# Neighbourhood attention on one core: position tables loaded in four pieces, the second image on GpSimd's queue, and a new order of the first work

## The chip, the cores and the metric

One core of a Trainium2 chip runs the whole kernel. The metric is device time in microseconds of that core, here the median of three runs. The core has a matrix engine (PE, with its weight loads as PEld), VectorE (DVE), ScalarE (ACT), GpSimd (POOL) and SyncE (SP), which work side by side, each through its own list of instructions in order. SP, ACT and POOL can also issue DMA transfers; a transfer's issue stands in the list of the engine that issues it.

## What is computed

Two images of 128 channels and 64 x 64 pixels, float32. After a group norm comes a block with neighbourhood attention (7 x 7 window, four heads of 32), then an attention over all 4096 tokens, then a long convolution by spectral filters. The change touches only the beginning of the first block. Cut to that:

```python
x = _gn(x)                                        # 32 groups, per image
y = _ln(x.transpose(0, 2, 3, 1), g1, be1)
qkv = (y @ qkv_w.T + qkv_b)                       # 3 x 4 heads x 32
attn = einsum('bnhwd,bnhwijd->bnhwij', q, Kw)     # 7 x 7 keys round each pixel
attn = attn + rpb[:, bih, biw][None]              # relative position, rpb is (4, 13, 13)
attn = softmax(attn over the 49 keys)
out = einsum('bnhwij,bnhwijd->bnhwd', attn, Vw)
...                                               # projection, two more norms, a small MLP, residuals
...                                               # attention over tokens, spectral filters
```

`rpb` holds, for each head, one number for each of 13 x 13 relative positions.

## The kernel before

**Tiling.** An image is cut into eight bands of eight rows (512 pixels); a band into eight tiles of 8 x 8 pixels, taken two at a time as four units u0 to u3. A unit computes, for each head, the scores of 2 x 64 pixels against a window of 14 x 14 = 196 keys (piece `S`, L505), adds a table and takes a minimum on DVE (piece `t`, L518), exponentials on ACT (piece `e`, L528), transposes the result on PE (`T`, L541), copies it out of PSUM (`c`, L548) and multiplies it with V on PE (`V`, L563). Two bands of keys and values must be there before the first scores.

**The table** (`tab`, L241) has, for six kinds of place in the image and four heads, 128 x 196 numbers: a mask (`mask`, loaded at L283) less the position numbers (`base`). `table` (L254) makes one of them; kind 0 is made on DVE, the others on POOL. `base` comes out of `flipped` (L246): `rev` holds, in 64 partitions, one for each pixel of a tile, the head's numbers shifted by the pixel's row and column; one matmul of 64 x 400 with a reversed identity turns the order of the partitions round, and ACT copies the result. `rev` is loaded straight from `rpb_pad`, a zero-padded copy of `rpb` in DRAM with rows of 128 numbers (`RPW`), by sixteen DMAs at L284 to L292: for each of the eight pixel rows one for heads 1 to 3 and one for head 0, all in runs of 20 numbers. POOL zeroes two parts of it first (L281, L282). `rev` lies in the space of `cm[0]`, `base` and `mask` in that of `tok[0]`; both are written with other things later.

**V.** ACT copies a band's V out of PSUM (piece `p.vc`, L470); SP stores it to DRAM in eight DMAs (`vd`, L475) and loads it back, as windows of 14 x 14 keys, in four DMAs for each unit (`windows`, L484 to L493). Those buffers (`vw`) are six units deep.

**The order.** Each engine's order is the order in which the program emits the pieces. Every piece of every band has a due time in `PLAN`, with 2300 between bands; the pieces are sorted by it. What comes first is written out by hand in `FIRST` (L72): its names get the times -1000, -999 and so on. `gn` is the group norm of the first image, `p.xg0` band 0's normalised pixels, `p.tok0` their transposes, `p.bn`, `p.pw`, `p.zd`, `p.nb`, `p.za`, `p.tr`, `p.zT` the layer norm, `p.q`, `p.k`, `p.v` the linears, `p.qT`, `p.kT`, `p.vc` their copies; `w` and `wd` prepare the weights, `f0` to `f3` are `flipped` of each head, `tab0` to `tab3` the tables of kind 0, `tab` those of kinds 1, 4 and 5. `behind` (L746) makes biases and weights that are used only behind the attention; its four steps lie at 150, 500, 850 and 1200 (L790). `second` (L793) loads the second image on ACT's queue, four DMAs of 512 KB, at 1000. The first image is loaded by SP in four DMAs at L126. The second image's own group norm begins at 2 x 2300 + 50 (L799).

Within a manual schedule the four compute engines keep this order; SP's DMAs follow the order of their program too.

Of the kernel before, what the change touches and what calls it, by code (L numbers as in the profile page):

```python
# [8 lines left out]
F32 = mybir.dt.float32  # L9
# [5 lines left out]
P = 128  # L15
# [5 lines left out]
HEADS, DH, KW = 4, 32, 7  # L21
# [9 lines left out]
W_QKV, W_PROJ, W_1, W_2, W_3 = 0, 384, 512, 640, 768  # L31
V_G1, V_BE1, V_G2, V_BE2, V_G3, V_BE3, V_G4, V_BE4, V_QB, V_KB, V_BL3 = range(11)
R_VB, R_PROJ, R_BL1, R_BL2 = range(4)
RPW = 128


QT, WN, NTAB = 8, 14, 20
# [2 lines left out]
BAND = QT * GW  # L40


RPR = NTAB + 1

# [23 lines left out]


FIRST = (  # L72
    "gn p.xg0 p.xg1 p.tok0 p.tok1 w p.bn0 p.bn1 p.pw0 p.pw1 p.zd0 p.nb0 p.za0 p.tr0 p.zd1 p.nb1 p.za1 wd p.xg2 p.zT0 f0"
    " p.tr1 f1 p.v0 p.q0 p.k0 p.zT1 p.vc0 p.qT0 tab0 p.kT0 f2 f3 tab p.v1 p.k1 p.q1 tab1 p.vc1 p.kT1 p.qT1 tab2 tab3"
).split()
PHW = P + TH

# [15 lines left out]
def kernel(  # L93
# [16 lines left out]
    nc = tc.nc  # L110
# [12 lines left out]
    xa = [xp.tile([P, T], F32, tag=f"xa{b}", name=f"xa{b}") for b in range(NB)]  # L123
    xin = x.rearrange("b c h w -> b c (h w)")
    for c in range(4):
# [3 lines left out]
    tt, tok, cm = [None, None], [None, None], [None, None]  # L129
# [4 lines left out]
    space = tok[0].rearrange("p n c -> p (n c)")  # L134
    base = space[:, 0 : HEADS * NTAB * NTAB].rearrange("p (h n m) -> p h n m", h=HEADS, n=NTAB)
    mask = space[:, HEADS * NTAB * NTAB : HEADS * NTAB * NTAB + 6 * KEYS].rearrange("p (c k) -> p c k", k=KEYS)
    rev = cm[0][0 : QT * QT, 0 : HEADS * RPR * NTAB].rearrange("p (h n m) -> p h n m", h=HEADS, n=RPR)

    ident = const.tile([P, P], F32, name="ident")
    make_identity(nc, ident)  # L140
# [4 lines left out]
        out=flip, in_=flip, compare_op=ALU.not_equal, fill=1.0, base=1 - QT * QT, pattern=[[0, 2], [1, QT * QT]],  # L145
# [73 lines left out]
    with l0a:  # L219
# [10 lines left out]
        vdram = l0a.enter_context(tc.tile_pool(name="l0_dram", bufs=1, space=bass.MemoryType.DRAM))  # L230
# [10 lines left out]
        tab = big.tile([P, 6, HEADS, KEYS], F32, name="tab")  # L241
        def l0_bank(kind=0):
            pool, tag = rings[kind]
            return pool.tile([P, 512], F32, tag=tag, name="bank")

        def flipped(h):  # L246
            pb = l0_bank()
            nc.tensor.matmul(
                pb[:, 0 : NTAB * NTAB], lhsT=flip.rearrange("p a q -> p (a q)"),
                rhs=rev[:, h, 0:NTAB].rearrange("p n m -> p (n m)"), start=True, stop=True,  # L250
            )
            nc.scalar.copy(base[:, h].rearrange("p n m -> p (n m)"), pb[:, 0 : NTAB * NTAB])

        def table(ci, h, eng):  # L254
            n0 = (6, 0, 3)[ci // 2]
            for hp, m0 in ((slice(0, 64), 6), (slice(64, P), 0)) if ci % 2 == 0 else ((slice(0, P), 3),):
                eng.tensor_tensor(
                    tab[hp, ci, h].rearrange("p (n m) -> p n m", m=WN),
                    mask[hp, ci].rearrange("p (n m) -> p n m", m=WN),
                    base[hp, h, n0 : n0 + WN, m0 : m0 + WN], ALU.subtract,  # L260
                )
# [9 lines left out]
            out=gavg, in_=gavg, compare_op=ALU.is_ge, fill=0.0, base=0,  # L271
# [3 lines left out]
            out=gavg, in_=gavg, compare_op=ALU.is_ge, fill=0.0, base=3,  # L275
            pattern=[[4, 32], [0, 4]], channel_multiplier=-1,
        )
        gavg = gavg.rearrange("p g r -> p (g r)")


        nc.gpsimd.memset(rev[:, 0].rearrange("p n m -> p (n m)"), 0.0)  # L281
        nc.gpsimd.memset(rev[:, HEADS - 1, NTAB], 0.0)  # L282
        nc.sync.dma_start(out=mask, in_=nc.inline_tensor(_window_masks(), "window_masks").ap())  # L283
        for r in range(QT):  # L284
            lo = 6 - min(r, 6)
            src = bass.AP(
                rpb_pad.tensor, (RPR + r - 6) * RPW + 50, [[1, QT], [RPW, (HEADS - 1) * RPR - r // 7], [1, NTAB]]
            )
            rows_ = rev[r * QT : (r + 1) * QT].rearrange("p h n m -> p (h n) m")
            (nc.scalar if r % 3 == 2 else nc.sync).dma_start(out=rows_[:, RPR : HEADS * RPR - r // 7], in_=src)  # L290
            src = bass.AP(rpb_pad.tensor, (lo + r - 6) * RPW + 50, [[1, QT], [RPW, RPR - lo], [1, NTAB]])
            nc.scalar.dma_start(out=rows_[:, lo:RPR], in_=src)  # L292
        wg = w_sb
        cb = wp.tile([P, 5], F32, name="cb")
        C_Q, C_K, C_V, C_1, C_3 = range(5)
# [38 lines left out]
        def group_norm(b):  # L334
            xb = xa[b]
            gst = mp.tile([P, 8, 6], F32, tag="gst", name="gst", bufs=1)
            gmv = mp.tile([P, 2], F32, tag="gmv", name="gmv", bufs=1)
            for c in range(8):
                nc.vector.bn_stats(gst[:, c, :], xb[:, c * 512 : (c + 1) * 512])
                if c % 2:  # L340
                    yield
            nc.vector.bn_aggr(gmv, gst.rearrange("p a s -> p (a s)"))
            yield
            gm = mp.tile([P, 1], F32, tag="gm", name="gm", bufs=2)
            gv = mp.tile([P, 1], F32, tag="gv", name="gv", bufs=1)
            pb = l0_bank()
            nc.tensor.matmul(pb[:, 0:1], lhsT=gavg, rhs=gmv[:, 0:1], start=True, stop=True)
            nc.vector.tensor_copy(gm, pb[:, 0:1])
            nc.vector.tensor_tensor(gv, gmv[:, 0:1], gm, ALU.subtract)
            nc.vector.tensor_tensor(gv, gv, gv, ALU.mult)  # L350
            nc.vector.tensor_tensor(gv, gv, gmv[:, 1:2], ALU.add)
            yield
            pb = l0_bank()
            nc.tensor.matmul(pb[:, 0:1], lhsT=gavg, rhs=gv, start=True, stop=True)
            grs = mp.tile([P, 1], F32, tag="grs", name="grs", bufs=2)
            rsqrt(grs, pb[:, 0:1], 1e-5)
            norms[b] = gm, grs
            yield
# [413 lines left out]
        events = []  # L772
        for k, (b, g) in enumerate(order):
            t = {}
            for name, at in PLAN.items():
                if name[0] == "k" and b == 0:
                    continue

                at = FIRST.index(f"{name}{k}") - 1000 if f"{name}{k}" in FIRST else at + k * PERIOD
                events.append((at, k, name, lambda f=pieces[name], t=t, b=b, g=g: f(t, b, g)))  # L780
        for name, f in (
            ("gn", lambda: [None for _ in group_norm(0)]), ("w", weights), ("wd", weights_kept),
            *((f"f{h}", lambda h=h: flipped(h)) for h in range(HEADS)),
            *((f"tab{h}", lambda h=h: table(0, h, nc.vector)) for h in range(HEADS)),
            ("tab", lambda: [table(ci, h, nc.gpsimd) for ci in (1, 4, 5) for h in range(HEADS)]),
        ):
            events.append((FIRST.index(name) - 1000, None, "", f))
        for i in range(8):
            events.append((2 * PERIOD + 600 * i, None, "", lambda ci=2 + i // 4, h=i % 4: table(ci, h, nc.gpsimd)))
        rest_ = behind()  # L790
        for i in range(4):
            events.append((150 + 350 * i, None, "", lambda: next(rest_)))
        def second():  # L793
            for c in range(4):
                nc.scalar.dma_start(out=xa[1][:, c * 1024 : (c + 1) * 1024], in_=xin[1, :, c * 1024 : (c + 1) * 1024])

        events.append((1000, None, "", second))

        gn1 = group_norm(1)  # L799
        for i in range(7):  # L800
# [597 lines left out]
def _window_masks():  # L1398

    import numpy as np  # L1400

    def seen(offset):

        q, k = np.arange(QT)[:, None], np.arange(WN)[None, :]
        lo = np.clip(offset + q - 3, 0, WN - KW)
        return (k >= lo) & (k < lo + KW)

    m = np.zeros((2, QT, QT, 6, WN, WN), np.float32)
    for ci in range(6):
        rows_ = seen((0, 6, 3)[ci // 2])  # L1410
        for ab in range(2):
            cols = seen(((0, 6), (3, 3))[ci % 2][ab])
            m[ab, :, :, ci] = np.where(rows_[:, None, :, None] & cols[None, :, None, :], 0.0, -MASKED)
    return m.reshape(P, 6, KEYS)
# [75 lines left out]
```

## Time and profile before

| | us |
|---|---|
| median of 3 runs | 2242.70 |
| lowest, highest | 2241.91, 2243.04 |
| the profiled execution | 2241.68 |
| its span in the profile | 2240.0 |
| PE busy | 2174.1 (97%) |
| PEld busy | 1344.1 (60%) |
| DVE busy | 940.5 (42%) |
| ACT busy | 780.6 (35%) |
| POOL busy | 276.2 (12%) |

The profiled execution lies 1.0 us below the median, and its span 1.7 us below its own time. The page of the profile gives busy times over the whole span, then the same in 40 slices, the DMA queues, the chain of work that ended last, and the costliest groups of instructions. A line of a group or of the timeline reads: start in us, duration in us, engine, source line, operation, output <- inputs with their shapes, the number of instructions, and in brackets the idle time of the engine just before and what ended it. "SPq" and "ACTq" are the DMA issues in an engine's own list; the time of a group of issues runs from the first to the end of the last, with waits between them. A table of stretches gives, for a stretch of time, its length and each engine's busy time in it with the number of instructions, then PE's granted clock as a share of full speed, the mean busy share of the 16 DMA engines and the GB/s that they moved.

The first 350 us or so are the neighbourhood attention of both images; it ends in the token attention of image 0, then come the rest of the attention and the filters.

### The profile page before, as it was taken

To read this page: it belongs to the slowest core of one execution; us is meant where nothing else is said; L and a number is where in the kernel's file an instruction comes from. 1 tells how busy PE (TensorE), PEld (TensorE's weight loads), DVE (VectorE), ACT (ScalarE), POOL (GpSimd) and SP (SyncE) were. 2 spreads that over 40 slices of the span, in tenths; PEclk is the share of its full clock that TensorE was granted. 3 is DMA by queue.
4 is the path that set the end of the run, shared out by engine and by line. 5 is a ranking of instruction groups with operands and counts; after the bars stand their busy time and mean duration, and the time that the engine had idled before them with its cause. 6 is when DMAs were issued, how large, how long until landed. Compare 5 with 4: busy or idle time off the path is not lost.

```text
span 2240.0 us, 31648 instructions
## 1 busy us (share of the span) xinstructions
PE 2174.1 (97%) x11888; PEld 1344.1 (60%) x11888; DVE 940.5 (42%) x3046; ACT 780.6 (35%) x1908; POOL 276.2 (12%) x353
## 2 busy tenths in 40 slices
PE   5899998999999999999999999999999999999998
PEld 3677765544454444544544447767677676767677
DVE  4799985434443346433333351222222323232323
ACT  2889883222332223222222332222322323232322
POOL 3377874200000000000000000000000000000000
PEclk8999998999999999999999999999999999999999
DMA  4222212011000016100000132212212122221101
GB/s 119 65 62 60 62 53 51 1 66 52 24 24 24 19 41 175 33 24 23 2 24 24 47 94 55 59 44 54 59 42 56 45 53 50 49 52 46 43 7 76
DMA packets 174810, 109.53 MB, mean 49 GB/s; under 512 B 26049, under 2 KB 159809, under 8 KB 174146
## 3 DMA queue, kind: packets, MB, share of 16 engines
q1 hardware_dynamic: 171818, 105.24, 18.0%
q10 hardware_dynamic: 2840, 2.27, 0.4%
q8 instruction: 94, 1.54, 0.3%
q14 instruction: 58, 0.48, 0.1%
HBM read 72.87 MB, written 34.60 MB: 48 GB/s over the span
## 4 chain that ended last, share of the span: by engine, by line
PE 86%; DVE 6%; POOL 3%; DMA 2%; ACT 1%; SPq 1%; issue 1%; DVEq 0%; ACTq 0%; POOLq 0%
PE acc L1316 25%; PE pc L1304 13%; PE bank L897 10%; PE own L925 10%; PE other L950 8%; PE bank L911 4%; PE py L1343 2%; PE bank L331 2%; PE bank L188 2%; PE bank L1042 2%; PE bank L1010 1%; PE bank L541 1%; DMA st<-in_m_minus_dram 1%; PE bank L505 1%; PE po L563 1%
## 5 line engine op out<-in xcount | busy, mean ns | idle before, releaser
L1305 DVE COPY y<-pc 128x512 f32<-128x512 f32 x320 | 221.4, 692 | 351.6 <-PE pc L1304 347.9
L904 ACT ACTIVATE e<-bank 128x512 f32<-128x512 f32 x288 | 171.8, 597 | 549.9 <-PE bank L897 415.2
L897 PE MATMUL bank<-cm 128*128 128x512 f32 x576 | 299.7, 605 | 1.4 <-DVE y L652 1.4
L1316 PE MATMUL acc<-y,mpl 128*128 128x256 f32 x1280 | 292.1, 382 | 0.0
L1316 PE MATMUL acc<-y,mmi 128*128 128x256 f32 x1280 | 288.0, 379 | 0.0
L1304 PE MATMUL pc<-ct,ut 64*128 64x512 f32 x1280 | 285.2, 595 | 0.9 <-issue 0.9
L1316 PEld LDWEIGHTS acc<-y,mpl 128*128 128x128 f32 x1280 | 238.2, 190 | 59.3 <-issue 29.6
L1316 PEld LDWEIGHTS acc<-y,mmi 128*128 128x128 f32 x1280 | 242.6, 190 | 32.6
L1305 ACT COPY y<-pc 128x512 f32<-128x512 f32 x320 | 204.5, 639 | 87.3 <-PE pc L1304 87.3
L925 PE MATMUL own<-et,tok 128*128 128x512 f32 x448 | 227.0, 593 | 1.9 <-DVE part L914 1.9
L950 PE MATMUL other<-e,tok 128*128 128x512 f32 x448 | 228.6, 592 | 0.0
L914 DVE CUSTOM_DVE_ANT_0 et<-bank,one 128x512 f32<-128x512 f32 x224 | 145.6, 687 | 166.0 <-PE bank L911 165.9
L1304 PEld LDWEIGHTS pc<-ct,ut 64*128 64x128 f32 x1280 | 121.5, 187 | 145.8 <-issue 140.6
L1322 ACT COPY ob<-acc 128x256 f32<-128x256 f32 x40 | 23.8, 595 | 431.2 <-PE acc L1316 431.2
L925 PEld LDWEIGHTS own<-et,tok 128*128 128x128 f32 x448 | 84.5, 190 | 109.8 <-issue 71.8
L950 PEld LDWEIGHTS other<-e,tok 128*128 128x128 f32 x448 | 85.1, 190 | 106.6 <-issue 105.7
L897 PEld LDWEIGHTS bank<-cm 128*128 128x128 f32 x576 | 96.2, 194 | 74.9 <-issue 46.1
L1355 DVE TENSOR_TENSOR xa<-py,xa 128x512 f32<-128x512 f32 x32 | 22.1, 691 | 281.4 <-PE py L1343 281.4
L911 PEld LDWEIGHTS bank<-ident,e 128*128 128x128 f32 x896 | 102.9, 141 | 56.5 <-issue 42.1
L160 POOL TENSOR_TENSOR ln_rs<-ln_rs,mhalf 128x4 f32<-128x4 f32 x24 | 24.3, 1011 | 848.0 <-DVE ln_rs L159 848.0
L528 ACT ACTIVATE p<-p,mn 128x196 f32<-128x196 f32 x256 | 114.4, 449 | 20.8 <-DVE mn L518 13.4
L911 PE MATMUL bank<-ident,e 128*128 128x128 f32 x896 | 117.3, 274 | 0.0
(199 smaller groups left out, 2311.1 us busy)
## 6 DMA issues: line engine op xcount, KB each, us to landing
ut<-us SPq DMA_DIRECT2D x80, 256.0 KB
us<-ub SPq DMA_DIRECT2D x64, 256.0 KB
vw<-vd SPq DMA_DIRECT2D x256, 49.0 KB
ct<-gs SPq DMA_DIRECT2D x160, 72.0 KB
ct<-gs SPq DMA_DIRECT2D x160, 64.0 KB
gs<-sum SPq DMA_DIRECT2D x20, 256.0 KB
vd<-v SPq DMA_DIRECT2D x128, 32.0 KB
st<-in_m_plus_dram SPq DMA_DIRECT2D x16, 256.0 KB
```

The source lines that it names most:

```text
L188: nc.tensor.transpose(ps[:, j * P : (j + 1) * P], src[:, j, :], ident)
L331: nc.tensor.matmul(pl, lhsT=wg[:, lo : lo + P], rhs=zT, start=True, stop=True)
L528: nc.scalar.activation(p, p, AF.Exp, bias=t[name + "mn"][:, h : h + 1], scale=-1.0, accum_out=t["den"][:, u, h : h + 1],)
L897: nc.tensor.matmul(ps, lhsT=cm[b][:, n * P : (n + 1) * P], rhs=cm[b][:, chunk(c)], start=True, stop=True)
L904: nc.scalar.activation(e, ps, AF.Exp, bias=0.0, scale=ASCALE, accum_out=part[:, n, c : c + 1])
L911: nc.tensor.transpose(pt[:, k * P : (k + 1) * P], es[k][:, m * P : (m + 1) * P], ident)
L914: nc.vector.tensor_tensor_reduce(et, pt, one, 1.0, 0.0, ALU.mult, ALU.add, part[:, n, a : a + 1])
L925: nc.tensor.matmul(own, lhsT=tok[b][:, n, :], rhs=e, start=first, stop=last)
L950: nc.tensor.matmul(other, lhsT=tok[b][:, 4 * CHUNKS[a] + j, :], rhs=es[j], start=(j == 0), stop=(j == 3))
L1304: nc.tensor.matmul(pc, lhsT=ut[fp, b, par, :], rhs=cv_[fp], start=True, stop=True)
L1305: (nc.scalar.copy if f else nc.vector.tensor_copy)(y[:, 4 * f : 4 * f + 4, :, par, b * 2 * FB + q : (b + 1) * 2 * FB : 2], pc.rearrange("p ...
L1316: nc.tensor.matmul(acc, lhsT=(mmi if l else mpl)[:, k, :], rhs=y[:, 1::2, k, ::-1, :] if l else y[:, 0::2, k, :, :], start=(l == 0 and k = ...
```

## The change

1. *Table loads.* The padded table has rows of 70 numbers instead of 128, and 22 rows for a head instead of 21. The six rows ahead of it are needed too, so that DRAM space `rpb` of (6 + 88) x 70 numbers is filled by two DMAs, DRAM to DRAM: its first six rows with the table's first six, as filler, then the whole table. Then one DMA for each head loads `rev[h]`: partition (row, column) reads 1350 numbers in one run from `row * 70 + column` on. The matmul of `flipped` picks 20 runs of 20 numbers out of them, with a step of 70. The four pieces of `rev` lie in `tt[0]` (heads 0 and 3) and `cm[0]` (heads 1 and 2). POOL's two memsets are gone. All six DMAs are on ACT's queue; before, six of the sixteen were on SP's.
2. *Second image.* `second` is issued from POOL's queue, as `x1` in `FIRST`, after `p.pw1`, and no longer from ACT's at 1000.
3. *Order.* `f0` and `f1` stand right after `w`, `f2` after `p.zT0`, `f3` after `p.tr1`; `tab` right after `f3`; `tab0` to `tab2` before `p.kT0`, `tab3` after it. The steps of `behind` lie at 900, 1200, 1500 and 1800.

```diff
-RPW = 128
+RPW = 70
-RPR = NTAB + 1
+RPR = NTAB + 2
+RLEN = (NTAB - 1) * RPW + NTAB

 FIRST = (
-    "gn p.xg0 p.xg1 p.tok0 p.tok1 w p.bn0 p.bn1 p.pw0 p.pw1 p.zd0 p.nb0 p.za0 p.tr0 p.zd1 p.nb1 p.za1 wd p.xg2 p.zT0 f0"
-    " p.tr1 f1 p.v0 p.q0 p.k0 p.zT1 p.vc0 p.qT0 tab0 p.kT0 f2 f3 tab p.v1 p.k1 p.q1 tab1 p.vc1 p.kT1 p.qT1 tab2 tab3"
+    "gn p.xg0 p.xg1 p.tok0 p.tok1 w f0 f1 p.bn0 p.bn1 p.pw0 p.pw1 x1 p.zd0 p.nb0 p.za0 p.tr0 p.zd1 p.nb1 p.za1 wd p.xg2"
+    " p.zT0 f2 p.tr1 f3 tab p.zT1 p.v0 p.q0 p.k0 p.vc0 p.qT0 tab0 tab1 tab2 p.kT0 tab3 p.v1 p.k1 p.q1 p.vc1 p.kT1 p.qT1"
 ).split()

-    rev = cm[0][0 : QT * QT, 0 : HEADS * RPR * NTAB].rearrange("p (h n m) -> p h n m", h=HEADS, n=RPR)
+    place = tt[0].rearrange("p n c -> p (n c)")[0 : QT * QT, 3 * P :]
+    rev = [place[:, 0 : NTAB * RPW], *(cm[0][0 : QT * QT, h * RLEN : h * RLEN + NTAB * RPW] for h in range(2))]
+    rev.append(place[:, NTAB * RPW : 2 * NTAB * RPW])

-                rhs=rev[:, h, 0:NTAB].rearrange("p n m -> p (n m)"), start=True, stop=True,
+                rhs=rev[h].rearrange("p (n w) -> p n w", w=RPW)[:, :, 0:NTAB], start=True, stop=True,

-        nc.gpsimd.memset(rev[:, 0].rearrange("p n m -> p (n m)"), 0.0)
-        nc.gpsimd.memset(rev[:, HEADS - 1, NTAB], 0.0)
         nc.sync.dma_start(out=mask, in_=nc.inline_tensor(_window_masks(), "window_masks").ap())
-        for r in range(QT):
-            lo = 6 - min(r, 6)
-            src = bass.AP(
-                rpb_pad.tensor, (RPR + r - 6) * RPW + 50, [[1, QT], [RPW, (HEADS - 1) * RPR - r // 7], [1, NTAB]]
-            )
-            rows_ = rev[r * QT : (r + 1) * QT].rearrange("p h n m -> p (h n) m")
-            (nc.scalar if r % 3 == 2 else nc.sync).dma_start(out=rows_[:, RPR : HEADS * RPR - r // 7], in_=src)
-            src = bass.AP(rpb_pad.tensor, (lo + r - 6) * RPW + 50, [[1, QT], [RPW, RPR - lo], [1, NTAB]])
-            nc.scalar.dma_start(out=rows_[:, lo:RPR], in_=src)
+        rpb = vdram.tile([(6 + HEADS * RPR) * RPW], F32, name="rpb")
+        flat = rpb_pad.rearrange("h r w -> (h r w)")
+        nc.scalar.dma_start(out=rpb[0 : 6 * RPW], in_=flat[0 : 6 * RPW])
+        nc.scalar.dma_start(out=rpb[6 * RPW :], in_=flat)
+        for h in range(HEADS):
+            src = bass.AP(rpb.tensor, rpb.offset + h * RPR * RPW + 50, [[RPW, QT], [1, QT], [1, RLEN]])
+            nc.scalar.dma_start(out=rev[h][:, 0:RLEN], in_=src)

+        def second():
+            for c in range(4):
+                nc.gpsimd.dma_start(out=xa[1][:, c * 1024 : (c + 1) * 1024], in_=xin[1, :, c * 1024 : (c + 1) * 1024])

-            ("tab", lambda: [table(ci, h, nc.gpsimd) for ci in (1, 4, 5) for h in range(HEADS)]),
+            ("x1", second), ("tab", lambda: [table(ci, h, nc.gpsimd) for ci in (1, 4, 5) for h in range(HEADS)]),

-            events.append((150 + 350 * i, None, "", lambda: next(rest_)))
-        def second():
-            for c in range(4):
-                nc.scalar.dma_start(out=xa[1][:, c * 1024 : (c + 1) * 1024], in_=xin[1, :, c * 1024 : (c + 1) * 1024])
-
-        events.append((1000, None, "", second))
+            events.append((900 + 300 * i, None, "", lambda: next(rest_)))
```

The matrix work is the same before and after, and so are the stores and window loads of V. Behind the first lines of the changed kernel its line numbers are one higher in the attention (L506 for the scores, L519, L529, L542, L564).

## The prediction

> **What bounds the kernel now.** I read the page first: PE is busy 2174.1 us of 2240.0 (97%), so a change that takes no matmul away can only win where PE is idle. The slices put PE's idle time at the head of the program. The table of stretches shows it:
>
> ```profile
> core 0: us, PE busy (x) PEld busy (x) DVE busy (x) ACT busy (x) POOL busy (x), PEclk, DMA share, GB/s
> ...
> 40.00:50.00 10.00, 8.55 (x54) 5.57 (x54) 6.61 (x34) 3.00 (x11) 5.03 (x7) 0.58 0.42 123
> 50.00:60.00 10.00, 4.94 (x44) 2.96 (x45) 0.88 (x2) 5.07 (x19) 0.00 (x0) 0.56 0.60 193
> 60.00:80.00 20.00, 18.27 (x325) 12.96 (x323) 13.15 (x66) 15.93 (x49) 5.13 (x7) 1.00 0.20 54
> ```
>
> From 50 to 60 us PE works 4.94 of 10 us, at a granted clock of 0.56. By the same table it works 20.00 of 20 from 140 us on. So time won before 60 us is kept if nothing between 60 and 140 us eats it. The timeline of ACT and PE shows who is late at 50 us:
>
> ```profile
> 46.35 0.45 ACT L405 ACTIVATE z<-bank,ln_nb,ln_rs 128x128 f32<-128x128 f32 x1
> ...
> 47.63 5.90 ACTq L795 DMA_DIRECT2D xa<-in_x_dram  x3
> ...
> 53.58 0.46 ACT L528 ACTIVATE p<-p,mn 128x196 f32<-128x196 f32 x1 [6.78 <-DMA vw<-vd]
> ...
> 55.06 1.95 PE L541 MATMUL bank<-ident,p 128*98 128x128 f32 x8 [5.77 <-ACT p L528]
> ...
> 58.65 0.67 PE L563 MATMUL po<-pT,vw 98*32 98x64 f32 x32
> ```
>
> ACT's exponentials (L528) need nothing of vw. But ACT's own queue stands in front of them: the second image's loads (L795). One issue takes 0.33 to 0.44 us, three take 5.90 because they wait. [...] The chain of waits has that load:
>
> ```profile
> 48.22 4.47 DMA vw<-vd
> ```
>
> Ahead of that lies the path through the position tables:
>
> ```profile
> 18.47 1.28 ACT L405 ACT_TABLE_LOAD   x1 [18.47 <-DVE ln_nb L394]
> ...
> 20.28 1.25 PE L188 MATMUL bank<-ident,z 128*128 128x128 f32 x4 [2.94 <-ACT z L405]
> ...
> 21.46 1.70 PE L248 MATMUL bank<-cm,flip 64*128 64x400 f32 x2
> ...
> 31.18 1.71 PE L248 MATMUL bank<-cm,flip 64*128 64x400 f32 x4
> ...
> 35.67 2.33 DVE L257 TENSOR_TENSOR tab<-tok 64x196 f32<-64x196 f32 x4
> ...
> 36.07 0.59 PE L505 MATMUL bank<-kT,qT 32*64 32x196 f32 x16
> ```
>
> One flip costs 1.70 us at 21 us and half of 1.71 at 31 us[...]. The first scores stand at 36.07, but DVE first makes tables (2.33), so that its first minimum (L518) starts at 39.25. Last, SP's queue:
>
> ```profile
> 28.49 10.98 SPq L475 DMA_DIRECT2D vd<-v  x16
> 39.51 21.37 SPq L492 DMA_DIRECT2D vw<-vd  x22
> 62.79 4.96 SPq L475 DMA_DIRECT2D vd<-v  x8
> 67.85 13.09 SPq L492 DMA_DIRECT2D vw<-vd  x16
> 81.03 4.96 SPq L475 DMA_DIRECT2D vd<-v  x8
> ```
>
> From 62.79 it never rests: a band costs 4.96 + 12.64 (the commonest run of 16) + 0.1 = 17.7 us of issuing, against 18.0 us between one band's first L563 and the next (129.22, 147.23, 165.25). SP is nearly as full as PE.
>
> [...] 410 GB/s at a share of 1.02 from 4 to 6 us. [...]
>
> **The change, part by part.** Times are of the profiled execution: 2241.68 us, span 2240.0; the median shown is 1.0 above it.
>
> (1) *Table loads.* Sixteen loads (406 KB in rows of 80 B, about 5200 rows) and two POOL memsets (0.44 + 0.11, not waited for later) go. Two DRAM copies (26 KB) and four loads of 64 rows of 5400 B (1.38 MB) come, all on ACT's queue. ACT now starts at about 0.8 instead of 2.29. Before shows no DRAM-to-DRAM copy; the first image's first piece lands 3.8 us after issue, so I take 4 us (2 to 6) for the copies: the loads start moving at about 6 us. By the 2 us stretches 1.4 of the first image's 2.1 MB is then in. The other 0.7 MB shares the engines with three table loads: at worst half rate, 0.7 MB / 0.41 = 1.7 us late; at best 0. I take **d = 1.2 us loss**. It shifts everything behind the group norm (L342, 9.83). [...] they must land by 15.5 + d (weights) and 24 (masks): 4.5 MB at 0.41 MB/us end at about 13, so this costs 0, and 1 us per us if that slack of 2.5 us went.
>
> (2) *Order of the first work.* The 1.28 us table load of ACT no longer waits for L394; it stands behind the last DMA issue at about 10 us: it leaves the path. Flips 0 and 1 move into PE's idle time: 17.1 to 20.5. ACT's two copies (0.49 each) now stand before z, so z starts at 21.05 instead of 19.77: 1.3 lost. Flips 2 and 3 take the places of 0 and 1 (cold), and nothing stands at 31.2 (1.7 won). PE: transposes 21.45, flip, transposes, flip to 27.2, v 29.2; [...] q and k 31.2, v 32.3, k and q 34.2, transposes 34.8. With d the first scores stand at **36.0** (before 36.07): gain 0. Bounds: clock early, 33.6; cold throughout, 39.
>
> (3) *Tables off DVE's path.* From scores to L563 was 58.65 - 36.07 = 22.6 us. Now DVE does statistics (0.89 + 0.38) and four minima (0.28 each), ending at +2.5; exponentials end at +3.6, eight transposes at +4.5. DVE then does a copy (0.69), z (0.71) and L753's two copies (0.9): +6. The minima of units 1 and 2 run to +8.5, second scores and the shifted bias products (four, 0.4 each) to +9.5, transposes and eight p transposes to +11.4, a linear 0.6: L563 at about **+12**, that is 48.0; +11.3 with PE warm, +13 cold. The moved steps of behind() cost PE the same; their DVE work (0.41 + 0.78 + 0.29) now lies near the first L563, where DVE idles for 9 us before.
>
> (4) *ACT's stall.* 6.78 us between 46.8 and 53.58 goes; it is inside the 22.6 of (3), not on top. PE gains 58.65 - 48.0 = **10.6 us**.
>
> (5) *What is late next: SP.* v0 is copied at about 31.05 (before 28.46), so 16 stores run 31.1 to 41.0 and vw loads start at 41.05 (before 39.51). Unit 0's four land near 46.5, before 48.0. 22 loads at 0.75 end at 57.5: v2's stores gain 62.79 - 57.5 = 5.3 only. Band 1's first L563 (75.03) needs two more loads after the stores: 67.85 + 1.5 + 2.4 to land = 71.8, slack 3.2. So its gain is at most 5.3 + 3.2 = **8.5**. SP at its pure 17.7 then gains 0.5 more each band (5.8, 5.9, 6.5 at the next three), with slacks of 4.0, 4.3, 3.1: caps of 9.8, 10.2, 9.6. PE, 18.27 of 20 busy there, can recover a little: I take **8.8**.
>
> (6) *Second image on POOL.* It is needed by its own group norm at 81 us: always in time. POOL issues it at 18.9 + d, ahead of the tables. No row has the price of a GpSimd DMA: bounds 0.4 us (an ACT issue) [...]; I take 1. Four end at 24; POOL's 16 table operations (9.9 us) wait for the last flip copy at about 29 anyway and end near 37, when band 2's rsqrt is due. [...]
>
> Sum: 2241.68 - 8.8 = 2232.9; plus 1.0 to the median: **2233.9**.
>
> **Rivals.** (A) As above, 2230 to 2238: chance 0.68. (B) SP's queue sets the pace fully and PE recovers nothing: 5.3 to 6.5 won, **2236.8**; the back-to-back queue speaks for it, the slack of 3 to 4 us before L563 against: 0.18. (C) One wait takes the other's place: d = 2.6 and scores cold at 39 + 1.4, L563 at +13 = 53.4[...]: 2.2 won, **2240.5**, within 0.2%: 0.09. (D) Slower: the table loads read one 26 KB region 64 times over. If they moved not at the 410 GB/s of 4 KB rows but at the 44 GB/s that the trace shows from 12 to 14 us with 80 B rows, 1.38 MB would take 31 us and the last land at 37; PE, in order, would stand at flip 3 (due 26.7) with v, q, k and scores behind. Below about 43 GB/s the whole gain is eaten; at 34 the last lands at 46, 19 us late: 48.0 + 19 = 67, **2251**. Rows of 5400 B speak against: 0.05. That the change doesn't do what it says: L795 and sixteen loads are gone from ACT's list, so no.
>
> **Numbers.** About 0.2% (4.5 us) is what a measurement here can tell from no change. Faster 0.86 (A, B), same 0.09 (C), slower 0.05 (D). Range 2229.5 to 2238.5: A's bounds (early clock with d = 0: 11 to 12; cold or POOL late: 6 to 7) and B; C and D stay out.
>
> **What would show it.** ACT without a gap before L529's fifth exponential; table load of ACT near 10 us; DVE's last image statistics 0 to 1.7 us late; first scores 34 to 39, first L564 near 48, with PE's clock not halved for 17 us; v2's stores near 57.5; the same distances from there on. Wrong if flips wait for DMA, if POOL's tables end after 41, or if L564 waits on vw.

## The result and the profile after

| | before | after |
|---|---|---|
| median | 2242.39 (8 runs) | 2235.70 (8 runs) |
| lowest, highest | 2240.02, 2243.73 | 2232.78, 2239.89 |
| the profiled execution | 2241.68 | 2236.08 |
| its span | 2240.0 | 2234.4 |

The ratio is 0.9973, with a 95% interval of 0.9964 to 0.9982: 6.1 us won, between 4.0 and 8.1. The forecast was 2233.9, in a range of 2229.5 to 2238.5; the sum for the profiled execution had been 2232.9, and it took 2236.08. Two thirds of the gain that was forecast came; where the rest stayed is the question of the experiments.

The same stretches as before, of the changed kernel:

```profile
core 0: us, PE busy (x) PEld busy (x) DVE busy (x) ACT busy (x) POOL busy (x), PEclk, DMA share, GB/s
...
40.00:50.00 10.00, 9.50 (x55) 6.25 (x54) 4.32 (x26) 5.99 (x21) 0.32 (x1) 0.53 0.21 60
50.00:60.00 10.00, 9.01 (x169) 6.77 (x169) 5.88 (x30) 6.46 (x21) 2.73 (x5) 0.96 0.24 67
60.00:80.00 20.00, 15.99 (x260) 10.99 (x259) 13.60 (x63) 14.63 (x48) 7.44 (x12) 0.95 0.22 60
```

PE now works 9.01 us from 50 to 60 instead of 4.94. But from 40 to 50 it is full at a clock of 0.53, and from 60 to 80 it works 15.99 us instead of 18.27: a part of the time won is given back there. The timeline of PE and ACT, and ACT's own issues:

```profile
8.09 0.67 ACTq L293 DMA_DIRECT2D tt<-rpb  x1
...
17.34 0.58 ACTq L293 DMA_DIRECT2D tt<-rpb  x1
17.96 1.28 ACT L256 ACT_TABLE_LOAD   x1 [17.96 <-DMA tt<-rpb]
...
41.62 0.46 ACT L529 ACTIVATE p<-p,mn 128x196 f32<-128x196 f32 x1 [0.47 <-DVE mn L519]
```

```profile
18.14 1.70 PE L252 MATMUL bank<-tt,flip 64*128 64x400 f32 x2
...
22.45 1.25 PE L192 MATMUL bank<-ident,z 128*128 128x128 f32 x4 [0.94 <-ACT z L406]
...
34.96 0.59 PE L506 MATMUL bank<-kT,qT 32*64 32x196 f32 x16
...
41.08 1.76 PE L506 MATMUL bank<-kT,qT 32*64 32x196 f32 x16 [0.50 <-DVE mn L519]
...
50.12 1.00 PE L564 MATMUL po<-pT,vw 98*32 98x64 f32 x32
...
67.05 0.54 PE L564 MATMUL po<-pT,vw 98*32 98x64 f32 x24
68.82 0.32 PE L564 MATMUL po<-pT,vw 98*32 98x64 f32 x8 [1.23 <-DMA vw<-vd]
```

ACT's fifth exponential starts at 41.62 instead of 53.58, and the gap of 6.78 us ahead of it is 0.47. The scores stand at 34.96 (36.07 before), the first V matmul at 50.12 (58.65). The same 16 matmuls of scores cost 0.59 us at 34.96 and 1.76 at 41.08, the second at a clock of 0.50 and with a wait inside. Last, a new wait: the first V matmul of band 1 breaks off after 24 of 32 and waits for a load of vw until 68.82. SP's queue:

```profile
30.65 9.95 SPq L476 DMA_DIRECT2D vd<-v  x16
40.65 17.18 SPq L493 DMA_DIRECT2D vw<-vd  x22
57.93 4.96 SPq L476 DMA_DIRECT2D vd<-v  x8
62.99 13.10 SPq L493 DMA_DIRECT2D vw<-vd  x16
```

v2's stores start at 57.93 instead of 62.79. SP never rests, and the wait at 68.82 lies on its way.

**How the lead runs.** The best measure of this kernel turned out to be the lead: by how much the start of the same V matmuls in a profile lies ahead of that of before. It keeps to 0.1 us over long stretches where PE is full, and steps where something costs time. The table has it for all kernels of the study, which are told below. Unit 1 is band 0's first (58.65 before), 7 band 1's third (80.64), 9 band 2's first (93.96), 33 image 1's first (201.34), 63 nearly the last (340.21); the end is that of the span (2240.0). Each row is one execution, and where PE's clock halves changes from one to the next: e6 and e8, which are the same up to band 1, differ by 0.7 us at unit 1 (in e8 the clock was half from 44.4 to 47.8 us, in e6 it was 1.00 from 40 to 60). Differences of that size between two rows prove nothing by themselves.

| kernel | unit 1 | 7 | 9 | 33 | 63 | end | ratio of times (95%) |
|---|---|---|---|---|---|---|---|
| after | 8.5 | 6.5 | 5.7 | 5.6 | 7.0 | 5.6 | 0.9973 (0.9964 to 0.9982) |
| e1 second image alone | 5.4 | 5.3 | 5.3 | 5.3 | 5.7 | 5.8 | 0.9967 (0.9955 to 0.9980) |
| e2 second image back | 1.8 | 0.4 | 0.4 | 0.4 | 2.4 | 3.3 | 0.9987 (0.9980 to 0.9993) |
| e3 old table loads | 4.4 | 4.2 | 4.2 | 2.4 | 4.3 | 5.4 | 0.9977 (0.9967 to 0.9987) |
| e4 split loads | 6.5 | 5.8 | 5.8 | 5.8 | 7.7 | 5.6 | 0.9966 (0.9955 to 0.9978) |
| e5 fillers | 10.1 | 5.2 | 4.3 | 3.0 | 5.7 | 4.2 | 0.9975 (0.9968 to 0.9982) |
| e6 split, fillers | 11.3 | 11.1 | 10.2 | 10.2 | 12.1 | 10.4 | 0.9951 (0.9939 to 0.9964) |
| e7 as e1, fillers | 8.5 | 7.1 | 6.3 | 6.3 | 8.0 | 7.9 | 0.9966 (0.9953 to 0.9978) |
| e8 as e6, more fillers | 10.6 | 10.4 | 10.4 | 10.4 | 10.7 | 7.8 | 0.9952 (0.9941 to 0.9964) |
| e9 as e1, split, fillers | 9.3 | 9.3 | 9.3 | 9.3 | 8.3 | 5.4 | 0.9960 (0.9948 to 0.9972) |
| e10 as e3, split, fillers | 9.0 | 8.7 | 7.3 | 7.3 | 7.8 | 7.4 | 0.9967 (0.9954 to 0.9980) |

The changed kernel's lead is 8.5 us at the first V matmul, 6.5 when band 1's first has waited for vw, 5.7 in band 2, and then stands still for 200 us.

### The profile page after: what moved, and what is told of

Same layout as the page of the kernel before. It is cut to its first block, busy times and chain, and to the rows that moved or that the text cites. A ratio compares the mean times of both kernels' runs of the same rounds, so it can differ in the third digit from the quotient of the medians.

```text
span 2234.4 us, 31639 instructions
## 1 busy us (share of the span) xinstructions
PE 2173.3 (97%) x11888; PEld 1344.7 (60%) x11888; DVE 940.7 (42%) x3046; ACT 781.1 (35%) x1908; POOL 278.1 (12%) x355
## 4 chain that ended last, share of the span: by engine, by line
PE 86%; DVE 6%; POOL 3%; DMA 2%; ACT 1%; issue 1%; SPq 1%; DVEq 0%; POOLq 0%; ACTq 0%
PE acc L1316 25%; PE pc L1304 13%; PE own L925 10%; PE bank L897 10%; PE other L950 8%; PE bank L911 4%; PE py L1343 2%; PE bank L332 2%; PE bank L192 2%; PE bank L1042 2%; PE bank L542 1%; PE bank L1010 1%; DMA st<-in_m_minus_dram 1%; PE bank L506 1%; ACT p L529 1%
## 5 line engine op out<-in xcount | busy, mean ns | idle before, releaser
L529 ACT ACTIVATE p<-p,mn 128x196 f32<-128x196 f32 x256 | 114.4, 449 | 12.9 <-DVE mn L519 12.4
```

The source lines that it names most:

```text
L529: nc.scalar.activation(p, p, AF.Exp, bias=t[name + "mn"][:, h : h + 1], scale=-1.0, accum_out=t["den"][:, u, h : h + 1],)
```

## The experiments

**e1: GpSimd's queue alone.** Theory: ACT's stall is what stood in front of the first V matmul. Rival: the tables on DVE's path and the order.

```diff
 kernel before
-    "gn p.xg0 p.xg1 p.tok0 p.tok1 w p.bn0 p.bn1 p.pw0 p.pw1 p.zd0
+    "gn p.xg0 p.xg1 p.tok0 p.tok1 w p.bn0 p.bn1 p.pw0 p.pw1 x1 p.zd0
...
-                nc.scalar.dma_start(out=xa[1][:, c * 1024 : (c + 1) * 1024]
+                nc.gpsimd.dma_start(out=xa[1][:, c * 1024 : (c + 1) * 1024]
...
+            ("x1", second),
-        events.append((1000, None, "", second))
```

> The kernel before with one part of the change alone: the second image's four loads go from ACT's queue at 1000 to POOL's queue behind p.pw1; table loads and order stay old. Theory (ACT's stall is what stood before the first V matmul, and GpSimd's queue alone takes it away): no 6.8 us gap of ACT before its fifth exponential; first V matmul (L563) at about 52 instead of 58.65, and after SP's share of about 1 us is lost again 5.5 to 6 us won, 2236.5 to 2237. Rival (the tables on DVE's path and the order are what counts, the stall is only hidden time): V at about 57, at most 2 us won, 2240.5 or more.

Measured: 2235.39 us, as much won as by the whole change. First V matmul at 53.23, 1.2 us later than the theory had it, while PE's clock was 0.50 throughout from 40 to 50 us and 0.82 to 60 (e7 tells what that costs). The gap of ACT is gone. The rival falls for this kernel; e9 and e10 come back to what tables and order are worth. And the changed kernel's start, 3.1 us earlier at the first V matmul, is worth 0.4 us of lead in band 2: something takes nearly all of those 3 us.

**e2: the other two parts without it.**

```diff
 changed kernel
-                nc.gpsimd.dma_start(out=xa[1][:, c * 1024 : (c + 1) * 1024]
+                nc.scalar.dma_start(out=xa[1][:, c * 1024 : (c + 1) * 1024]
...
-            ("x1", second),
+        events.append((1000, None, "", second))
```

> The changed kernel with the second image back on ACT's queue at 1000: new table loads and new order, without GpSimd's queue. Theory (the issue of the third piece waits again for the twelfth vw load, which SP now issues near 49 and which lands near 53.4): ACT stands still before its exponentials until about 54, first V matmul near 59, time within 1 us of the kernel before, 2241.5 to 2243. Rival (order and tables win by themselves): V near 55 or earlier and 3 us or more won, 2239 or less.

The timeline of ACT of this kernel:

```profile
41.35 0.36 ACTq L797 DMA_DIRECT2D xa<-in_x_dram  x1
45.19 6.56 ACTq L797 DMA_DIRECT2D xa<-in_x_dram  x3
51.80 0.46 ACT L529 ACTIVATE p<-p,mn 128x196 f32<-128x196 f32 x1 [9.70 <-DMA xa<-in_x_dram]
```

ACT is held in its own queue for longer than before, 9.70 us between two of its operations (6.78 before), and by the second unit the lead is 0.4 us. So the stall comes back with the loads in ACT's queue, as the theory had it; which transfer the third issue waited for, this timeline doesn't show. The total, 2239.17, is 3.0 us below that of before and fits neither forecast; of the profile's 3.3 us, 2.8 arise behind the first image's attention: 0.6 at the start of image 1, 1.3 between 331 and 340 us, 0.9 later. Most of that is not e2's own doing. Nearly all kernels of the study gain the same 0.5 to 0.6 us at the start of image 1, and most gain 1.2 to 1.5 between 331 and 340, where the profile of before ran two groups of V matmuls at half clock (1.08 us instead of 0.65). That the median of 21 runs lies 3.0 us lower too is not explained by one profile (see "What stays open").

**e3: old table loads in the new order.** The two copies and four loads go, the sixteen loads and two memsets come back.

```diff
 changed kernel
-RPW = 70
+RPW = 128
...
-            nc.scalar.dma_start(out=rev[h][:, 0:RLEN], in_=src)
...
+            (nc.scalar if r % 3 == 2 else nc.sync).dma_start(out=rows_[:, RPR : HEADS * RPR - r // 7], in_=src)
...
+            nc.scalar.dma_start(out=rows_[:, lo:RPR], in_=src)
```

> The changed kernel with the old sixteen table loads and the two memsets: the second image stays on POOL's queue, the order stays new. Theory (the new loads are of no use to the end; they cost the first image 0.9 us and flips wait for neither form for long): within 1 us of the changed kernel, 2234.7 to 2236.7; first scores 0 to 1 us earlier if the old rows land by 18 us. Rival (the new order needs the new loads, since flips 0 and 1 stand before the layer norm): flip 0 at 20 us or later, scores 2 us or more later, 1.5 us or more of the gain gone at the end, 2237.2 or more.

The timeline of PE:

```profile
20.27 3.00 PE L249 MATMUL bank<-cm,flip 64*128 64x400 f32 x4 [2.24 <-DMA cm<-in_rpb_pad_dram]
24.22 1.25 PE L189 MATMUL bank<-ident,z 128*128 128x128 f32 x4 [0.94 <-ACT z L405]
```

The early flips wait for the old rows until 20.27, 2.1 us longer than for the new ones, and the layer norm's transposes start 1.8 us later. The first V matmul comes 4.1 us later than in the changed kernel, of which the clock has a share (0.50 until about 54). The medians differ by 1.2 us, which the intervals don't separate; the leads at unit 9 are 4.2 and 5.7. The flips' wait is the rival's; the size at the end lies between the two. That the lead falls further, to 2.4 at unit 33, comes from SP's queue again: in band 5 the last eight V matmuls of the first unit wait 1.43 us for vw, until 145.05.

**e4: eight window loads off SP.** Units 2 and 3 of band 0 are loaded from POOL's queue, which is idle then (for 16.87 us up to 57.18 in the changed kernel).

```diff
 changed kernel
-                windows(b, g - 1)
+                windows(b, g - 1, range(2) if (b, g) == (0, 1) else range(4))
+        events.append((160, None, "", lambda: windows(0, 0, (2, 3), nc.gpsimd)))
```

> The changed kernel with eight of SP's first 22 window loads (units 2 and 3 of band 0) issued from POOL behind its tables. Theory (the gain of 8.5 us at the first V matmul is cut to 5.7 because SP is late: v2's stores start at 57.9 and the first V matmul of band 1 waits until 68.8 for vw): stores of v2 near 52, no wait for vw at 68, 1.5 to 2 us more won than by the changed kernel, near 2234. Rival (PE's half clock at 78 to 82 us and its idle time there take it, SP isn't the limit): the same as the changed kernel within 0.5 us.

Measured: 2235.52, the same as the changed kernel. This doesn't clear SP, because the run didn't reach it: PE's clock stayed at half until 53 us (0.50 from 40 to 50, 0.84 from 50 to 60), the first V matmul came at 52.16, v2 was computed late and its stores waited for it until 56.96. No V matmul waits for vw, and the lead keeps at 5.8 from band 0 on. The step at band 1 is gone, but there was nothing left to win from it. So two limits lie next to each other, and one has to be lifted to see the other.

**e5: PE kept busy.** Filler matmuls whose result nobody reads go into PE's idle time behind the first scores.

```diff
 changed kernel
+        def warm(n):
+            pw = l0_bank(1)
+            for _ in range(n):
+                nc.tensor.matmul(pw, lhsT=ident, rhs=w_sb[:, 0:512], start=True, stop=True)
+        events += [(0.5, None, "", lambda: warm(2)), (1000, None, "", lambda: warm(1))]
```

> The changed kernel with three filler matmuls of 128 x 512 whose result nobody reads, two behind the first scores and one among the second scores, in PE's idle time from 36 to 41 us. Theory (PE's clock, halved from 41 to 51 us, is what made the first V matmul come at 50.1 instead of 48): no halved clock before 60 us, first V matmul at 46 to 47.5. What reaches the end depends on SP: if its queue is the limit from there on, V of band 1 waits at 68 to 69 as before and at most 1 us more is won than by the changed kernel (2234.7 or more); rival (the clock alone is the limit, SP isn't): about 3 us more, near 2232.5. Third possibility: the fillers don't hold the clock, and the time is the changed kernel's plus 0 to 1 us.

```profile
65.11 0.54 PE L564 MATMUL po<-pT,vw 98*32 98x64 f32 x24
68.53 0.38 PE L564 MATMUL po<-pT,vw 98*32 98x64 f32 x8 [2.89 <-DMA vw<-vd]
68.84 2.08 PE L332 MATMUL bank<-zT,w_sb 128*128 128x512 f32 x2
```

The clock was half from 44.8 to 48.2 only, and the lead at the first V matmul grew to 10.1. Then SP's load came at 68.53, within 0.3 us of where it came in the changed kernel, PE stood still for 2.89 us, and its clock halved again behind that (0.50 from 70 to 72 us): the two matmuls of L332 cost 2.08 us instead of 1.13. The lead fell to 5.2, and to 3.0 later. The whole run is 2236.76, no better. The clock alone is not the limit; SP is, once the clock is lifted. The first V matmul came at 48.51, later than the theory's 47.5, since three fillers didn't hold the clock throughout.

**e6: both.** The changed kernel with e4's and e5's edits:

```diff
+        events.append((160, None, "", lambda: windows(0, 0, (2, 3), nc.gpsimd)))
...
+        events += [(0.5, None, "", lambda: warm(2)), (1000, None, "", lambda: warm(1))]
```

> Both edits together: the fillers, and eight of SP's first 22 window loads on POOL. Theory (with PE at full clock SP is the next limit, so each edit needs the other): first V matmul at 46 to 47.5, v2's stores at about 52 to 54, no wait for vw in band 1, 3 to 5 us more won than by the changed kernel, 2231 to 2232.5. Rival (neither the clock nor SP matters behind 60 us, since band 0's own tail sets PE's pace there): the same as the changed kernel within 1 us.

PE and SP of this kernel:

```profile
47.37 0.65 PE L564 MATMUL po<-pT,vw 98*32 98x64 f32 x32
...
63.97 0.65 PE L564 MATMUL po<-pT,vw 98*32 98x64 f32 x32
```

```profile
39.99 11.04 SPq L493 DMA_DIRECT2D vw<-vd  x14
51.72 4.96 SPq L476 DMA_DIRECT2D vd<-v  x8
```

2231.32 us (2230.83 to 2232.11), the fastest of the study: a clock of 1.00 from 40 to 60 us, first V matmul at 47.37, v2's stores at 51.72, band 1's first V matmul in one piece at 63.97, a lead of 11.1 in band 1. The same fillers are worth -2.6 us of lead at unit 33 without the split and +4.3 with it (5.6 to 3.0; 5.82 to 10.16). The split is worth 0.2 at half clock and 7.1 with the fillers. That is what two limits in a row look like, and neither edit alone shows it. The measured times agree, if less sharply: e6's interval (0.9939 to 0.9964) lies clear of that of the fillers alone and ends where the changed kernel's begins, but overlaps that of the split alone (0.9955 to 0.9978).

**e7: fillers with the old order.** e1 with three fillers behind the first scores and one later.

```diff
 e1
+        events += [(0.5, None, "", lambda: warm(3)), (1000, None, "", lambda: warm(1))]
```

> The kernel with the second image on POOL's queue alone (old table loads, old order), with the same fillers, here three behind the first scores and one among the second. Theory (the new order brought the first V matmul only 3 us forward, because half clock stretched the same matmuls in both): V at about 50, and the distance to the changed kernel with fillers, 2 to 3 us at V, shows what the order is worth when PE is at full speed; time 2233 to 2235. Rival (the tables on DVE's path no longer matter once ACT is free): first V and total within 1 us of the changed kernel with fillers.

```profile
66.51 0.54 PE L563 MATMUL po<-pT,vw 98*32 98x64 f32 x24
68.24 0.32 PE L563 MATMUL po<-pT,vw 98*32 98x64 f32 x8 [1.18 <-DMA vw<-vd]
```

V at 50.14, 1.6 us behind that of e5, with the clock at 1.00; and the same wait for SP at 68.24. The lead falls from 8.5 to 7.1 to 6.3, as in the changed kernel, whose V stood at 50.12 for another reason. The total of 2234.91 is even lower than e5's: what the order brings earlier, SP's queue turns into a longer wait (2.89 us in e5, 1.18 here) and a further stretch of half clock (0.50 from 70 to 72 us in e5, 1.00 in e7).

**e8: fillers in the second pause too.** e6 with two more fillers in band 1.

```diff
 e6
+        events += [(PERIOD + at, None, "", lambda: warm(1)) for at in (2700, 2900)]
```

> The kernel with fillers and split window loads, and two more fillers of 128 x 512 in PE's pauses of band 1 (0.8 and 1.2 us, at 71 and 72.5 us), after which its clock was halved from 73.6 to 76.4 us. Theory (the pauses halve the clock, and the halved clock cost the 0.9 us that the lead fell there, from 11.1 to 10.2): clock 1.00 through, lead over the kernel before still 11 us at band 2's first V matmul, 0.5 to 1 us less in all, near 2230.5. Rival (the fillers push the matmuls behind them as far as the full clock gains): no change within 0.3 us at band 2's first V matmul.

The timeline of PE in that pause, first of e6, then of this kernel:

```profile
71.88 0.64 PE L542 MATMUL bank<-ident,p 128*98 128x128 f32 x4 [0.80 <-DVE mn L519]
73.70 1.11 PE L327 MATMUL bank<-ident,rb 128*128 128x128 f32 x4 [1.18 <-POOL rb L581]
74.61 1.92 PE L542 MATMUL bank<-ident,p 128*98 128x128 f32 x8
```

```profile
73.00 1.02 PE L803 MATMUL bank<-w_sb,ident 128*128 128x512 f32 x2
74.35 0.66 PE L327 MATMUL bank<-ident,rb 128*128 128x128 f32 x4 [0.32 <-POOL rb L581]
74.84 1.04 PE L542 MATMUL bank<-ident,p 128*98 128x128 f32 x8
```

Behind two pauses of 0.80 and 1.18 us eight transposes cost 1.92 us. With the fillers they cost 1.04, and the lead doesn't step at band 2 (10.41, 10.41; e6 11.06, 10.19). The theory holds in its place. The total, 2231.94, is not below e6's: in this profile the clock was half from 44.4 to 47.8, where the same instructions ran at full clock in e6, and 2.9 us of lead went behind 340 us.

**e9 and e10: what order and loads are worth when both limits are lifted.** e9 is e7 with the split; e10 is e3 with fillers and split as in e6:

```diff
 e7 and e3
-                windows(b, g - 1)
+                windows(b, g - 1, range(2) if (b, g) == (0, 1) else range(4))
+        events.append((160, None, "", lambda: windows(0, 0, (2, 3), nc.gpsimd)))
```

> The second image on POOL's queue with the old table loads and the old order, with fillers and split window loads. Against the same with the new loads and order (V at 47.37, 2231.3): theory (new loads and order are worth what they bring forward the first V matmul, once neither clock nor SP takes it back): V near 50, about 2.8 us later than with them, and 2 to 3 us more in all, 2233 to 2234.5. Rival (the tail behind 60 us catches up whatever comes earlier): within 1 us of 2231.3.

> The changed kernel with the old sixteen table loads, with fillers and split window loads: order and POOL's queue new, loads old. Theory (flips 0 and 1 stand early in PE's list and must wait for the old loads, which keep PE 1.5 to 2 us longer than the new ones): first V matmul at 49 to 50, 1.5 to 2.5 us more than with the new loads, 2233 to 2234. Rival (the loads' form makes no difference): V at 47 to 48 and within 1 us of 2231.3.

First V matmuls at 49.40 and 49.67. At unit 7, ahead of the second pause, the leads are 9.3 and 8.7 against e6's 11.1, at unit 33 9.3 and 7.3 against 10.2: e6 and e10 lose 0.9 and 1.4 to half clock behind that pause (0.50 from 74 to 76 us and from 76 to 82), e9, whose clock was 1.00 there, nothing. So by these profiles new order and new loads together are worth 1.8 us of lead where it arises and 0.9 further on, less than the 2.8 that I expected. With the old loads the new order costs 0.6 against the old one (1.9 further on), since the flips stand at the front of PE's list and wait 2.94 us for their rows: by the leads, the new order pays with the new loads only. The medians (2235.06 and 2235.36) are 3.7 and 4.0 above e6's, which is more than both theories had; the intervals of the three overlap. The profiled execution of e9 was the slowest of its five (2236.29) and loses 3.9 us of lead between unit 33 and the end, where e6 wins 0.2: from 300 to 370 us its mean clock was 0.85, e6's 0.93. The leads up to unit 33 are free of that, and so they are the better measure of the parts; what the parts are worth in the whole time lies somewhere between 0.9 and 3.7 us and is not settled.

**What stays open.** All profiles lose or win 1 to 4 us between 300 and 370 us, where the attention of image 1 ends and the token attention begins. The timeline of PE in e9 there:

```profile
356.44 0.33 PE L188 MATMUL bank<-ident,tok 128*128 128x128 f32 x1 [3.67 <-POOL tok L702]
...
359.37 1.92 PE L902 MATMUL bank<-cm 128*128 128x512 f32 x2
361.07 1.91 PE L600 MATMUL bank<-w_sb,att 128*128 128x128 f32 x8
362.78 1.87 PE L902 MATMUL bank<-cm 128*128 128x512 f32 x2
364.49 1.02 PE L930 MATMUL own<-e,tok 128*128 128x512 f32 x2
```

PE waits for POOL, and then three groups run at half clock (a mean of 0.76 from 355 to 360 us, 0.55 from 360 to 365); in e2 it was one and a half (1.92, 1.58, 1.02). The mean clock from 300 to 370 us was 0.90 in before and in the changed kernel, 0.95 in e2, e3 and e7, which all win 1.6 to 2.9 us of lead behind unit 33, and 0.85 in e9, which loses 3.9; but e8 loses 2.6 at 0.90, so that the mean alone doesn't account for it. The clock of the runs that were only timed points the same way: within the 29 runs of before that were timed beside e1, time and mean clock have a correlation of -0.75, within the 20 of e5 -0.78, within the eight of the changed kernel -0.58, each time with about 1 us more for 0.001 less clock. So the spread of the changed kernel (2232.8 to 2239.9) goes with its clock. Whether the clock makes it, or the pauses that lie ahead of its halving, is open: no run was made that holds the clock there.

## Why the prediction was right, and where its sizes were off

The likeliest case came, in its range: ACT's stall goes, PE's start gains (8.5 us, where 10.6 were forecast), and SP's queue caps what is kept. The range was wide enough to take in rival B as well. Its steps in turn:

1. *Table loads.* d was put at 1.2 us (0 to 1.7); DVE's aggregate behind the last statistics started 0.88 later (L343 at 10.71 instead of L342 at 9.83). The first of the four loads was issued at 8.09 rather than near 6, and the last waited until 17.34; as the first flips are due at 18, it did no harm. The new loads didn't move at 410 GB/s: the table of stretches has 173 GB/s from 10 to 20 us. Rival D's direction was right, its size far off.
2. *Order of the first work.* Forecast and measured: flips 18.0 and 18.14, z 21.93 and 21.93, transposes 22.3 and 22.45 (all with d = 0.88), scores 35.7 and 34.96, 0.7 earlier than summed. ACT's table load came at 17.96 and not near 10, behind its last DMA issue, and is hidden there all the same. Warm and cold in these sums are readings of durations alone: in the kernel before a flip took 1.70 us at 21.46 and 0.86 at 31.18, while the table of stretches has a granted clock of 1.00 from 18 to 36 us. What made the later one shorter is not shown.
3. *From scores to V.* Put at 12 us, 13 with PE cold; it took 15.2. This is one term that was mis-sized: PE's clock was half from 40.6 to 50.9, which the range allowed for at 1 us and which costs 3. With the clock up, e6 has 47.37 - 35.59 = 11.8, fillers included: the count of steps agrees. This miss didn't reach the end, since SP's cap (step 5) lay below it: e5 brought the first V matmul forward by 1.6 us, and SP's load came 0.3 us earlier.
4. *ACT's stall.* As forecast; e1 and e2 show that it is nearly the whole of what is kept: at band 2 the lead is 5.3 us with this part alone, 0.4 without it and 5.7 with all three. The chain of waits of the kernel before has eleven of SP's window loads being issued from 39.51 on, then the transfer of the twelfth, which lands at 52.69, and behind it the third piece's issue:

```profile
52.69 0.02 issue
52.71 0.33 ACTq L795
```

5. *SP.* The limit was right and v2's stores were forecast at 57.5 (57.93 measured). The other mis-sized term is "two more loads after the stores: 1.5 + 2.4". SP's list doesn't stand in the order in which the pieces are emitted: with 16 loads for each band, the first 22 are those of band 0 and six of band 1, ahead of v2's stores. And the load that band 1's first unit waits for is not the second behind these stores but the fifth. The chain of waits of the changed kernel has four issues, then the transfer of the next load:

```profile
62.99 0.79 SPq L493
...
63.88 0.77 SPq L493
64.71 0.73 SPq L493
65.49 0.73 SPq L493
66.26 2.52 DMA vw<-vd
68.82 0.32 PE po L564 x8
```

From the first issue to the matmul it is 5.83 us, not 3.9 (3.27 until the fifth issue starts, 2.52 until its data are there); 5.92 in e5 and 5.99 in e7. Put into the profile of before, 67.85 + 5.9 = 73.75, against the last eight of 32 matmuls at 75.03 + 0.49 (three quarters of 0.65): a slack of 1.8 instead of 3.2. The cap is then 4.9 + 1.8 = 6.7 instead of 8.5, and 6.5 was measured.
6. *Second image on POOL.* Four issues took 2.41 us, 0.60 each, where I took 1 and an ACT issue had taken 0.33 to 0.44; POOL's tables ended at 36.51 (37). Rival C's 2.2 us had time lost on POOL taken off, which no run shows.

So 8.8 became 5.6: 6.5 by SP's cap, less 0.9 for a second stretch of half clock at band 1, which the prediction had not seen and e8 takes away. The recovery of 0.3 that I gave PE didn't come. One of the prediction's own signs of being wrong did come: L564 waits on vw, 1.23 us in band 1. But that sign contradicts the prediction's own step 5, whose cap of 8.5 below a start of 10.6 already means such a wait. Rival B (SP sets the pace, 5.3 to 6.5 won) describes the changed kernel better than A in its size; but its premise, SP sets the pace fully, is not right for all bands, since in e6 the lead keeps at 10.2 with SP's later bands as they were.

## What to carry to other kernels

In these traces an issue that had to wait held its engine, and with it all that was queued behind (ACT for 6.78 us before, for 9.70 in e2); move such an issue to an idle engine's queue first, since here it was worth nearly the whole of the gain (5.3 of 5.7 us of lead at band 2). A gain ahead of a full queue is capped by that queue (6.7 us by the count above, 6.5 measured): count the issues up to the very transfer that the consumer's last instruction needs, in the order of the queue's own list, and try the cure of each limit together with that of the next, because alone they measured as nothing here (2235.52 and 2236.76 us against 2235.70, together 2231.32). A pause of PE costs more than itself where the clock halves behind it (0.9 us of lead in e6, behind pauses of 0.80 and 1.18 us).

## What the runs showed of the hardware

Where PE's granted clock halved in these profiles, it went from 1.00 to 0.50 and back. Two stretches of half a microsecond in the changed kernel, in which it changed:

```profile
40.50:41.00 0.50, 0.07 (x8) 0.00 (x0) 0.37 (x4) 0.50 (x2) 0.00 (x0) 0.65 0.29 66
50.50:51.00 0.50, 0.50 (x28) 0.45 (x20) 0.50 (x2) 0.00 (x0) 0.00 (x0) 0.61 0.09 27
```

A mean of 0.65 over the first puts the change at 40.65, 0.61 over the second the change back at 50.89: 10.2 us. The same reading gives 13.6 us in e1 (39.90 to 53.53) and 3.4 in e5 (44.76 to 48.18): three, four and one times 3.4 us. What sets these lengths, no run here shows. Work alone didn't bring the clock back at once: PE was busy 10.00 of 10 us from 42 to 52 by the table of stretches, and got its clock back only at 50.9. Nor was PE without work ahead of a halving: in the 3.4 us before it PE was busy 2.64 us in the changed kernel (37.24 to 40.65) and 1.79 us in e6 (69.87 to 73.29). How long a pause it takes isn't shown either: behind pauses of 0.80 and 1.18 us e6's clock halved at 73.29, behind one of 1.18 us e7's stayed at 1.00 (68 to 72 us).

The issue of a 512 KB load held POOL for 0.60 us. The transfer landed a median of 7.0 us after its issue, with four of them on the way. Between the end of the second issue of the small copies from DRAM to DRAM and the issue of the first load that reads them lay 5.3 us (2.84 to 8.09), while the first image was on its way (a piece of it landed at 8.04); how much of that was the copies' own time, the trace doesn't show.
